# Graph attention layer 0: the three score rows through DRAM instead of TensorE transposes, and ScalarE in source order

## The chip, the cores and the metric

The kernel runs on one core of a Trainium2 chip. A core has TensorE (matmuls, written PE in the profile), VectorE (DVE), ScalarE (ACT), GpSimd (POOL) and SyncE (SP, which here only issues DMA transfers). The metric is the device time of one execution in microseconds; before the change it is 3209.09 us, the median of three runs (3208.32 to 3210.53).

## The reference

The input is x of shape 32 x 512 x 512 in float32 and one 512 x 512 adjacency matrix shared by all 32 batch elements. Two layers follow each other, and each is added to its input and layer-normalised:

```
layer 0:  h = x W                                    (512 x 256)
          e[i,k] = leakyrelu(h[i].a0 + h[k].a1, 0.2) - 1e9 (1 - adj[i,k])
          x = layernorm(x + concat(softmax(e) h, h))
layer 1:  q, k, v = x Wq' + bq, x Wk' + bk, x Wv' + bv     (8 heads of 64)
          scores = q k' / 8, minus infinity where adj is 0
          x = layernorm(x + (softmax(scores) v) Wo' + bo)
```

What matters here is layer 0: its 512 x 512 score matrix is a sum of a column and a row, built from two numbers per node, h.a0 ("self") and h.a1 ("neighbour").

## The kernel before

A batch element is called a problem below. A tile has 128 partitions; the 512 nodes of a problem are four blocks of 128 nodes (index i or j), so a vector over the nodes is a column of shape 128 x 4. Everything is float32 but the masks, which are bfloat16.

For each problem b the loop at the end of the function goes through four head pairs (hp 0 to 3). In each, `head_scores` (called for the four query blocks) multiplies q and k into PSUM (`ps`, L547), VectorE adds the mask and takes the row maximum in one instruction (`minus_max`, L287), and ScalarE takes the exponential (L556). `head_blocks` transposes 32 x 32 blocks on VectorE (L302), takes the reciprocal of the sums (L565), writes these to DRAM (`d_tot`, L567), reads them back broadcast (`inv`, L570, issued by GpSimd) and issues 16 transfers on SyncE that finish the transposition (`pt` from `t`, L319). `head_values` of the head pair before then multiplies with v (`pav`, L582) and VectorE scales the result (`ot`, L590). `project_two` makes q and k of two head pairs (`pw`, L457, with seven products in place of eight, and ScalarE copies `p1`, `p5`, `p7`, `u2` into buffers of the tag "p"), `project_v` makes v (`pv`, L239, copied out at L530), and `finish` multiplies with Wo (`pf`, L603).

Between those pieces of layer 1 for problem b stand the pieces of layer 0 for b + 1 and b + 2:

- `l0_project(b + 2, i)`, in hp 3: h of one block of nodes, with self and neighbour as its first two columns (`ph`, L239; copied by ScalarE at L339).
- `l0_scores(b + 1)`, in hp 0 between query blocks 1 and 2. `row_of` (L326) turns the column of neighbours into a row that stands on all partitions: four TensorE transposes of a column broadcast to 128 x 128, into PSUM (`pn`). VectorE reduces it four times with mask0 (`junk`, L287), and two tiny instructions make `most` (L360, L361), an upper bound of each node's scores. Four more transposes make the row of selfs (`pself`). ScalarE takes leaky ReLU of row plus column (L366), and GpSimd adds the transposed mask (L370).
- `l0_rows(b + 1)`, in hp 0 behind `head_values`: four transposes make the row of `most` (`pl`).
- `l0_weights(b + 1)`: VectorE subtracts that row (L383), ScalarE takes the exponential (L384).
- `l0_values(b + 1, i)`, in hp 1: the weights times h (`po`, L391), and so on to the layer norm and the transposed x1 of the next problem.

The order of the work on TensorE, SyncE and VectorE is that of the source, by this line:

```
ctx.enter_context(tc.manual_schedule(engines={mybir.EngineType.PE, mybir.EngineType.SP, mybir.EngineType.DVE}))
```

ScalarE's and GpSimd's instructions are ordered by a planner of the framework, by its own estimates. An engine works through its queue in order and waits at an instruction whose inputs or buffers aren't ready. A pool gives each tag a number of buffers (`bufs`); a tile waits until one is released. In PSUM, four banks (tag "m") serve all products but the scores, which have four of their own (tag "s"). Tag "p" has ten buffers, "inv" two.

Problem 0's layer 0 runs before the loop, in a startup that also makes the masks (`masks0`: `maskf` in float32 and from it `mask0`), scales and sums the weights (`weight_sums`) and makes the first x1 (`x1_first`). There GpSimd and VectorE share the mask adds.

Of the kernel before, what the change touches and what calls it, by code (L numbers as in the profile page):

```python
# [26 lines left out]
def kernel(  # L27
# [51 lines left out]
    NB = N // P  # L79
    FC = F // P  # L80
    OC = F1 // P
    NP = H // 2
# [11 lines left out]
    ps_m = ctx.enter_context(tc.tile_pool(name="ps_m", bufs=4, space=bass.MemoryType.PSUM))  # L94
    ctx.enter_context(tc.manual_schedule(engines={mybir.EngineType.PE, mybir.EngineType.SP, mybir.EngineType.DVE}))

# [88 lines left out]
    def masks0():  # L185
        maskf = first[:, 4 * F :].rearrange("p (c n) -> p c n", c=NB)
        for c in range(NB):
            nc.vector.tensor_scalar(
                maskf[:, c, :], adj_sb[:, c, :], -1.0, -MASK0, ALU.add, ALU.mult
            )  # L190
            nc.vector.tensor_scalar(
                mask0[:, c, :], maskf[:, c, :], MASK0_MAX / MASK0, None, ALU.mult
            )
        for j in range(NB):
            pm = ps_m.tile([P, N], F32, name=f"pm_{j}", tag="m")
            for i in range(NB):
# [44 lines left out]
    def psum(name):  # L241
        return ps_m.tile([P, N], F32, name=name, tag="m")
# [98 lines left out]
    def l0_add_h(b):  # L341

        h_sb, z = st["h", b], st["x1", b]
        for i in range(NB):
            nc.gpsimd.tensor_tensor(
                z[:, i, F1:], z[:, i, F1:], h_sb[:, i, 2 : F1 + 2], ALU.add
            )

    def l0_scores(b):


        h_sb = st["h", b]
        pn = psum(f"pn_{b}")
        row_of(lambda i: h_sb[:, i, 1:2], pn)
        least = small.tile([P, NB], F32, name=f"least0_{b}", tag="least0", bufs=2)
        for i in range(NB):
            junk = prob.tile([P, N], F32, name=f"junk_{b}_{i}", tag="p", bufs=10)
# [3 lines left out]
        nc.vector.scalar_tensor_tensor(most, most, ALPHA, most, ALU.mult, ALU.max)  # L361
        pself = psum(f"pself_{b}")
        row_of(lambda i: h_sb[:, i, 0:1], pself)
        et = prob.tile([P, NB, N], F32, name=f"et_{b}", tag="et", bufs=1)
        for j in range(NB):
            nc.scalar.activation(  # L366
                et[:, j, :], pself, AF.Prelu, bias=h_sb[:, j, 1:2], alpha=ALPHA
            )
            engine = nc.vector if b == 0 and j >= 2 else nc.gpsimd
            engine.tensor_tensor(et[:, j, :], et[:, j, :], mask0t[:, j, :], ALU.add)  # L370
        st["l0", b] = et, most

    def l0_rows(b):
        _, most = st["l0", b]
        pl = psum(f"pl_{b}")
        row_of(lambda i: most[:, i : i + 1], pl)
        st["pl", b] = pl

    def l0_weights(b):
        et, _ = st["l0", b]  # L380
        pl = st.pop(("pl", b))
        for j in range(NB):
            nc.vector.tensor_tensor(et[:, j, :], et[:, j, :], pl, ALU.subtract)  # L383
            nc.scalar.activation(et[:, j, :], et[:, j, :], AF.Exp)  # L384
# [63 lines left out]
    def project_two(b, s):  # L448
# [30 lines left out]
        def copy(ps, name):  # L479
            t = prob.tile([P, N], F32, name=f"{name}_{b}_{s}", tag="p", bufs=10)  # L480
            nc.scalar.copy(t, ps)
            return t
# [50 lines left out]
    def head_scores(b, hp, i):  # L533
# [17 lines left out]
        for j in range(2):  # L551
            name = f"{b}_{hp}_{i}_{j}"
            p = prob.tile([P, N], F32, name=f"p_{name}", tag="p", bufs=10)
            least = small.tile([P, 1], F32, name=f"least_{name}", tag="least", bufs=6)
# [6 lines left out]
    def head_blocks(b, hp):  # L561
# [5 lines left out]
        nc.sync.dma_start(d.rearrange("j p i -> p j i"), total)  # L567
        inv = act.tile([P, P, NB], F32, name=f"inv_{b}_{hp}", tag="inv", bufs=2)
        for j in range(2):
# [73 lines left out]
    l0_add_h(0)  # L643
    l0_rows(0)
    l0_weights(0)
# [16 lines left out]
    l0_project(1, 2)  # L662
    l0_project(1, 3)
    x1_sums(0, nc.vector)
    project_v(0, 0)
# [3 lines left out]
    for b in range(B):  # L669
        more = b < B - 1  # L670
        for hp in range(NP):
# [27 lines left out]
            else:  # L699
# [4 lines left out]
                if b + 2 < B:  # L704
                    for i in range(NB):
                        l0_project(b + 2, i)
                if b == 0:
                    project_v(1, 0)
# [113 lines left out]
```

## Time and profile before

The profile is of one execution, of 3209.49 us, whose instructions span 3207.7 us.

| | busy us | share of the span | instructions |
|---|---|---|---|
| TensorE matmul | 3163.1 | 99% | 12216 |
| TensorE weight load | 1806.1 | 56% | 12216 |
| VectorE | 2451.1 | 76% | 5665 |
| ScalarE | 1332.1 | 42% | 3026 |
| GpSimd | 759.1 | 24% | 869 |

| what | count | busy us, or time to landing |
|---|---|---|
| `pn`, `pself`, `pl` transposes (L326) | 128 each | 20.8, 19.2, 21.7 |
| leaky ReLU (L366) | 128 | 76.4 |
| VectorE's subtraction of the row (L383) | 128 | 79.2 |
| `pt` from `t`, 128 KB, SyncE | 2048 | 3.4 to land |
| `d_tot` from `tot`, 4 KB, SyncE | 128 | 2.1 to land |
| `inv` from `d_tot`, 128 KB, GpSimd | 256 | 3.8 to land |

The 16 DMA engines were busy about half of the time, and moved 139 GB/s in the mean. The granted TensorE clock was 0.995 of full speed.

How to read it: an engine's line names the source line, the engine, the operation, what it writes and reads ("out<-in", buffer numbers left out), and shapes as partitions x elements. Lines of a timeline begin with the start and the length in us from the start of the span; what stands in brackets at their end is idle time ahead of the instruction and what ended it. TensorE's instructions overlap, so its cost is read from one start to the next. Each logical float32 matmul stands as two instructions.

### The profile page before, as it was taken

To read this page: it belongs to the slowest core of one execution; us is meant where nothing else is said; L and a number is where in the kernel's file an instruction comes from. 1 tells how busy PE (TensorE), PEld (TensorE's weight loads), DVE (VectorE), ACT (ScalarE), POOL (GpSimd) and SP (SyncE) were. 2 spreads that over 40 slices of the span, in tenths; PEclk is the share of its full clock that TensorE was granted. 3 is DMA by queue.
4 is the path that set the end of the run, shared out by engine and by line. 5 is a ranking of instruction groups with operands and counts; after the bars stand their busy time and mean duration, and the time that the engine had idled before them with its cause. 6 is when DMAs were issued, how large, how long until landed. Compare 5 with 4: busy or idle time off the path is not lost.

```text
span 3207.7 us, 41188 instructions
## 1 busy us (share of the span) xinstructions
PE 3163.1 (99%) x12216; PEld 1806.1 (56%) x12216; DVE 2451.1 (76%) x5665; ACT 1332.1 (42%) x3026; POOL 759.1 (24%) x869
## 2 busy tenths in 40 slices
PE   7999999999999999999999999999999999999997
PEld 5555555556556555555565565555555655655543
DVE  5788777877777877778777778877787777788775
ACT  3444443434444444434344444444343444444432
POOL 1322222221222222222222222222222122222210
PEclk9999999999999999999999999999999999999999
DMA  5565555555556555555555555555555555555554
GB/s 148 129 157 127 139 141 150 129 144 143 142 129 152 148 127 137 143 150 128 140 146 141 129 150 149 127 139 141 150 129 145 142 141 129 152 146 128 125 137 115
DMA packets 226094, 446.12 MB, mean 139 GB/s; under 512 B 81680, under 2 KB 84240, under 8 KB 225872
## 3 DMA queue, kind: packets, MB, share of 16 engines
q1 hardware_dynamic: 213408, 409.65, 50.5%
q0 software_dynamic: 12464, 33.84, 4.0%
q8 instruction: 99, 1.62, 0.2%
q14 instruction: 123, 1.01, 0.1%
HBM read 108.27 MB, written 34.08 MB: 44 GB/s over the span
## 4 chain that ended last, share of the span: by engine, by line
PE 95%; DVE 1%; SPq 1%; DMA 0%; issue 0%; ACT 0%; DVEq 0%; ACTq 0%
PE pw L457 25%; PE ps L547 15%; PE pav L582 14%; PE pv L239 14%; PE pf L603 13%; PE ph L239 7%; PE po L391 7%; SPq L319 1%; PE pl L326 1%; PE pn L326 1%; DVE t L302 0%; PE pself L326 0%; DMA pt<-t 0%; DVE p L287 0%; DVE x1t_b L302 0%
## 5 line engine op out<-in xcount | busy, mean ns | idle before, releaser
L556 ACT ACTIVATE p<-p,least 128x512 f32<-128x512 f32 x1024 | 725.9, 710 | 485.1 <-DVE least L287 416.4
L287 DVE CUSTOM_DVE_ANT_0 p<-ps,mask 128x512 f32<-128x512 f32 x1024 | 643.0, 684 | 314.0 <-PE ps L547 314.0
L302 DVE STREAM_TRANSPOSE t<-p 128x512 f32<-128x512 f32 x1024 | 621.8, 674 | 0.0
L547 PE MATMUL ps<-qk 64*128 64x512 f32 x2048 | 511.6, 615 | 2.4 <-DVE least L287 2.4
L582 PE MATMUL pav<-pt,v 128*64 128x512 f32 x2048 | 467.7, 598 | 5.3 <-DMA pt<-t 2.7
L603 PE MATMUL pf<-wo_sb,ot 128*128 128x512 f32 x1024 | 459.6, 602 | 5.6 <-DVE ot L590 5.6
L239 PE MATMUL pv<-wv_sb,x1t 128*128 128x512 f32 x1024 | 451.3, 593 | 0.0
L570 POOL DMA_DIRECT2D inv<-d_tot x256 | 134.4, 528 | 1296.2 <-DMA d_tot<-tot 712.2
L603 PEld LDWEIGHTS pf<-wo_sb,ot 128*128 128x128 f32 x1024 | 190.0, 191 | 272.4 <-issue 264.4
L547 PEld LDWEIGHTS ps<-qk 64*128 64x128 f32 x2048 | 177.8, 186 | 265.3 <-issue 207.5
L582 PEld LDWEIGHTS pav<-pt,v 128*64 128x64 f32 x2048 | 136.5, 136 | 321.1 <-issue 250.2
L239 PEld LDWEIGHTS pv<-wv_sb,x1t 128*128 128x128 f32 x1024 | 190.1, 191 | 216.0 <-issue 215.9
L239 PE MATMUL ph<-w_sb,xt 128*128 128x258 f32 x1024 | 236.9, 389 | 5.0 <-ACT x1t L422 4.7
L391 PE MATMUL po<-h,et 128*128 128x257 f32 x1024 | 232.6, 385 | 1.6 <-issue 1.6
L239 PEld LDWEIGHTS ph<-w_sb,xt 128*128 128x128 f32 x1024 | 194.8, 193 | 57.0 <-DVE mv L253 22.0
L258 ACT ACTIVATE rstd<-mv,eps 128x4 f32<-128x4 f32 (+1 forms) x70 | 20.8, 297 | 489.3 <-DVE mv L253 487.2
L391 PEld LDWEIGHTS po<-h,et 128*128 128x128 f32 x1024 | 193.4, 191 | 51.8 <-issue 25.4
L370 POOL TENSOR_TENSOR et<-et,mask0t 128x512 f32<-128x512 f32 x126 | 141.6, 1156 | 304.0 <-ACT et L366 304.0
L446 POOL TENSOR_TENSOR x<-x,bo_sb 128x512 f32<-128x512 f32 x128 | 158.4, 1269 | 190.4 <-DVE x1t_b L302 170.6
L493 DVE SCALAR_TENSOR_TENSOR qk<-pw,bqs_sb,p 128x256 f32<-128x256 f32 x128 | 61.6, 481 | 184.2 <-PE pw L457 116.7
L556 ACT ACTIVATION_READ_ACCUMULATOR p<-p,least 128x1 f32 x1024 | 191.2, 187 | 0.0
L252 DVE BATCH_NORM_STATS2 stats<-x 128x6 f32<-128x512 f32 x256 | 177.5, 693 | 13.9
(99 smaller groups left out, 3762.2 us busy)
## 6 DMA issues: line engine op xcount, KB each, us to landing
pt<-t SPq DMA_DIRECT2D x2048, 128.0 KB, 3.4
x<-in_x_dram SPq DMA_DIRECT2D x32, 1024.0 KB, 5.8
inv<-d_tot POOLq DMA_DIRECT2D x256, 128.0 KB, 3.8
xt<-in_xt_dram SPq DMA_DIRECT2D x31, 1024.0 KB, 5.4
x1t<-x1t_b SPq DMA_DIRECT2D x496, 64.0 KB, 2.0
out_dram<-x SPq DMA_DIRECT2D x31, 1024.0 KB, 4.3
d_tot<-tot SPq DMA_DIRECT2D x128, 4.0 KB, 2.1
xt<-in_xt_dram SPq DMA_DIRECT2D x4, 256.0 KB, 7.4
```

Of the source, the lines that this page charges most:

```text
L239: nc.tensor.matmul(ps, lhs(c), rhs(c), start=(c == 0), stop=(c == FC - 1))
L252: nc.vector.bn_stats(stats, z[:, i, :])
L287: nc.vector.tensor_tensor_reduce(out=out, in0=scores, in1=mask, scale=-1.0, scalar=MIN_INIT, op0=ALU.add, op1=ALU.min, accum_out=least,)
L302: nc.vector.transpose(t[:, :, :, i, :].rearrange("p r c q -> p c r q"), src.rearrange("p (c r k) -> p c r k", r=4, k=G),)
L370: engine.tensor_tensor(et[:, j, :], et[:, j, :], mask0t[:, j, :], ALU.add)
L391: nc.tensor.matmul(po, et[:, j, i * P : (i + 1) * P], h_sb[:, j, 2:], start=(j == 0), stop=(j == NB - 1),)
L446: nc.gpsimd.tensor_tensor(z[:, i, :], z[:, i, :], bo_sb, ALU.add)
L457: nc.tensor.matmul(ps[:, k * half : (k + 1) * half], weights(k, c), moving(c), start=start and k == 0 and c == 0, stop=c == FC // 2 - 1, s ...
L547: nc.tensor.matmul(ps, qk[rows, 0, i * P : (i + 1) * P], qk[rows, 1, :], start=True, stop=True)
L556: nc.scalar.activation(p, p, AF.Exp, bias=least, scale=-1.0, accum_out=total[:, j, i : i + 1])
L582: nc.tensor.matmul(po[j * D : (j + 1) * D, :], st["v", b, c][:, head * D : (head + 1) * D], pt[:, :, j, c, :, :].rearrange("p g i q -> p g ...
L603: nc.tensor.matmul(ps, st["ot", b, c][:, i * P : (i + 1) * P], wo_sb[:, c, :], start=(c == 0), stop=(c == FC - 1),)
```

## The change

For problems 1 to 31 the three rows no longer come from TensorE:

- `l0_columns(b)`, new, called right behind the four `l0_project(b, i)`: ScalarE copies the two columns of h into `att` (128 x 2 x 4), SyncE writes them to DRAM (`d_att`) in pieces of 16 bytes (four node blocks beside each other for one partition), and SyncE reads them back broadcast to all partitions into `rows` (128 x 2 x 512, 512 KB). The row's order is therefore q i, partition first, and no longer i q.
- `l0_scores(b)` takes `pn` and `pself` from `rows`. `mask0` is stored with its columns in the order q i, so that VectorE reads neighbours and mask alike from one end to the other; the leaky ReLU reads the selfs with a step of four elements and writes in the old order. At its end `most` is written to DRAM (`d_most`, 512 single numbers) and read back broadcast into `row` (128 x 512, 256 KB), both on SyncE.
- Problem 0 keeps its transposes, with those of `pn` written in the new order, `pself` made ahead of the reductions and `pl` at the end of `l0_scores`. `l0_rows` is gone.
- `l0_weights(b + 1)` stands ahead of `l0_add_h(b + 1)` in hp 0.
- ScalarE joins the engines whose order is that of the source.
- Tag "p" has nine buffers in place of ten, and "inv" one in place of two.

```diff
-    ctx.enter_context(tc.manual_schedule(engines={mybir.EngineType.PE, mybir.EngineType.SP, mybir.EngineType.DVE}))
+    in_order = {
+        mybir.EngineType.PE, mybir.EngineType.SP, mybir.EngineType.DVE,
+        mybir.EngineType.Activation,
+    }
+    ctx.enter_context(tc.manual_schedule(engines=in_order))
...
             nc.vector.tensor_scalar(
-                mask0[:, c, :], maskf[:, c, :], MASK0_MAX / MASK0, None, ALU.mult
+                mask0[:, c, :].rearrange("p (q i) -> p i q", i=NB),
+                maskf[:, c, :].rearrange("p (i q) -> p i q", i=NB),
+                MASK0_MAX / MASK0,
+                None,
+                ALU.mult,
             )
...
+    def l0_columns(b):
+
+        h_sb = st["h", b]
+        att = small.tile([P, 2, NB], F32, name=f"att_{b}", tag="att", bufs=2)
+        nc.scalar.copy(att, h_sb[:, :, 0:2].rearrange("p i k -> p k i"))
+        d = dram.tile([2, P, NB], F32, name=f"d_att_{b}", tag="datt")
+        nc.sync.dma_start(d.rearrange("k p i -> p k i"), att)
+        rows = prob.tile([P, 2, P, NB], F32, name=f"rows_{b}", tag="rows", bufs=1)
+        nc.sync.dma_start(rows, d.partition_broadcast(P))
+        st["rows", b] = rows
+
     def l0_scores(b):
 
 
         h_sb = st["h", b]
-        pn = psum(f"pn_{b}")
-        row_of(lambda i: h_sb[:, i, 1:2], pn)
+        if b == 0:
+            pself, pn = psum("pself"), psum("pn")
+            for i in range(NB):
+                nc.tensor.transpose(
+                    pn.rearrange("p (q i) -> p i q", i=NB)[:, i],
+                    h_sb[:, i, 1:2].to_broadcast([P, P]),
+                    ident,
+                )
+            row_of(lambda i: h_sb[:, i, 0:1], pself)
+        else:
+            rows = st.pop(("rows", b))
+            pself = rows[:, 0].rearrange("p q i -> p i q")
+            pn = rows[:, 1].rearrange("p q i -> p (q i)")
...
-        pself = psum(f"pself_{b}")
-        row_of(lambda i: h_sb[:, i, 0:1], pself)
         et = prob.tile([P, NB, N], F32, name=f"et_{b}", tag="et", bufs=1)
         for j in range(NB):
+            e = et[:, j, :] if b == 0 else et[:, j, :].rearrange("p (i q) -> p i q", i=NB)
             nc.scalar.activation(
-                et[:, j, :], pself, AF.Prelu, bias=h_sb[:, j, 1:2], alpha=ALPHA
+                e, pself, AF.Prelu, bias=h_sb[:, j, 1:2], alpha=ALPHA
             )
...
-    def l0_rows(b):
-        _, most = st["l0", b]
-        pl = psum(f"pl_{b}")
-        row_of(lambda i: most[:, i : i + 1], pl)
-        st["pl", b] = pl
+        if b == 0:
+            row = psum("pl")
+            row_of(lambda i: most[:, i : i + 1], row)
+        else:
+            d = dram.tile([N], F32, name=f"d_most_{b}", tag="dmost")
+            with nc.allow_non_contiguous_dma(reason="512 numbers"):
+                nc.sync.dma_start(d.rearrange("(i p) -> p i", p=P), most)
+            row = prob.tile([P, N], F32, name=f"row_{b}", tag="row", bufs=1)
+            nc.sync.dma_start(row, d.partition_broadcast(P))
+        st["l0", b] = et, row
...
-        inv = act.tile([P, P, NB], F32, name=f"inv_{b}_{hp}", tag="inv", bufs=2)
+        inv = act.tile([P, P, NB], F32, name=f"inv_{b}_{hp}", tag="inv")
...
+    l0_columns(1)
...
+                    l0_columns(b + 2)
...
-                if more:
-                    l0_rows(b + 1)
-                else:
+                if not more:
                     project_v(b, 1)
                 project_v(b, 2)
                 project_v(b, 3)
                 if more:
+                    l0_weights(b + 1)
                     l0_add_h(b + 1)
-                    l0_weights(b + 1)
```

Left out of the diff are the same change of `bufs` from 10 to the constant 9 (PB) at three further places and the use of `row` for `pl` in `l0_weights`.

More of the change, by code (lines that the diff above doesn't have):

```diff
@@ L80 @@
     FC = F // P
+    PB = 9
     OC = F1 // P
@@ L347, in l0_add_h @@
             )
+    def l0_columns(b):
[7 more added lines that the diff above has]
+        st["rows", b] = rows
     def l0_scores(b):
         h_sb = st["h", b]
-        pn = psum(f"pn_{b}")
-        row_of(lambda i: h_sb[:, i, 1:2], pn)
+        if b == 0:
[11 more added lines that the diff above has]
+            pn = rows[:, 1].rearrange("p q i -> p (q i)")
         least = small.tile([P, NB], F32, name=f"least0_{b}", tag="least0", bufs=2)
         for i in range(NB):
-            junk = prob.tile([P, N], F32, name=f"junk_{b}_{i}", tag="p", bufs=10)
+            junk = prob.tile([P, N], F32, name=f"junk_{b}_{i}", tag="p", bufs=PB)
             minus_max(junk, pn, mask0[:, i, :], least[:, i : i + 1])
@@ L370, in l0_scores @@
             engine.tensor_tensor(et[:, j, :], et[:, j, :], mask0t[:, j, :], ALU.add)
-        st["l0", b] = et, most
-    def l0_rows(b):
-        _, most = st["l0", b]
-        pl = psum(f"pl_{b}")
-        row_of(lambda i: most[:, i : i + 1], pl)
-        st["pl", b] = pl
+        if b == 0:
[8 more added lines that the diff above has]
+        st["l0", b] = et, row
     def l0_weights(b):
-        et, _ = st["l0", b]
-        pl = st.pop(("pl", b))
+        et, row = st["l0", b]
         for j in range(NB):
-            nc.vector.tensor_tensor(et[:, j, :], et[:, j, :], pl, ALU.subtract)
+            nc.vector.tensor_tensor(et[:, j, :], et[:, j, :], row, ALU.subtract)
             nc.scalar.activation(et[:, j, :], et[:, j, :], AF.Exp)
@@ L479, in copy @@
         def copy(ps, name):
-            t = prob.tile([P, N], F32, name=f"{name}_{b}_{s}", tag="p", bufs=10)
+            t = prob.tile([P, N], F32, name=f"{name}_{b}_{s}", tag="p", bufs=PB)
             nc.scalar.copy(t, ps)
@@ L552, in head_scores @@
             name = f"{b}_{hp}_{i}_{j}"
-            p = prob.tile([P, N], F32, name=f"p_{name}", tag="p", bufs=10)
+            p = prob.tile([P, N], F32, name=f"p_{name}", tag="p", bufs=PB)
             least = small.tile([P, 1], F32, name=f"least_{name}", tag="least", bufs=6)
@@ L643 @@
     l0_add_h(0)
-    l0_rows(0)
     l0_weights(0)
```

## The prediction

> **What bounds the kernel now.** I read the busy shares first, then the chain that ended last, then TensorE's timeline over one problem (one of the 32 batch elements) in mid-kernel.
>
> ```profile
> PE 3163.1 (99%) x12216; PEld 1806.1 (56%) x12216; DVE 2451.1 (76%) x5665; ACT 1332.1 (42%) x3026; POOL 759.1 (24%) x869
> ...
> PE 95%; DVE 1%; SPq 1%; DMA 0%; issue 0%; ACT 0%; DVEq 0%; ACTq 0%
> ```
>
> TensorE carries 95% of the chain. A repeated group in that chain (the output projection `pw` of the second half) comes back every 98.02 us (2843.55, 2941.57), through almost the whole kernel. So a microsecond off TensorE per problem is a microsecond off the kernel, unless a partner then comes late. The timeline of TensorE (start, length, line, operation) where the rows are made:
>
> ```profile
> 1433.84 1.99 PE L547 MATMUL ps<-qk 64*128 64x512 f32 x8
> 1435.76 0.65 PE L326 MATMUL pn<-ident,h 128*128 128x128 f32 x4
> 1436.24 0.60 PE L326 MATMUL pself<-ident,h 128*128 128x128 f32 x4
> 1436.68 7.03 PE L239 MATMUL pv<-wv_sb,x1t 128*128 128x512 f32 x16
> 1443.64 1.99 PE L547 MATMUL ps<-qk 64*128 64x512 f32 x8
> 1445.56 3.65 PE L582 MATMUL pav<-pt,v 128*64 128x512 f32 x16
> 1449.14 0.65 PE L326 MATMUL pl<-ident,most 128*128 128x128 f32 x4
> 1449.63 7.03 PE L239 MATMUL pv<-wv_sb,x1t 128*128 128x512 f32 x16
> 1456.59 1.99 PE L547 MATMUL ps<-qk 64*128 64x512 f32 x8
> 1458.51 7.21 PE L391 MATMUL po<-h,et 128*128 128x257 f32 x32
> 1465.65 1.99 PE L547 MATMUL ps<-qk 64*128 64x512 f32 x8
> 1467.57 3.65 PE L582 MATMUL pav<-pt,v 128*64 128x512 f32 x16
> ```
>
> No idle time is noted on any of them; starts, not lengths (they overlap), give the cost: pn and pself 1436.68 - 1435.76 = 0.92 us, pl 1449.63 - 1449.14 = 0.49 us, together 1.41 us a problem.
>
> **The skill.** SBUF — State Buffer, section "Door 1", says that an fp32 access which touches each 16-byte line only once pays a penalty. The trace agrees: L590 reads `inv` at that step and takes 1019 ns, against 689 ns for L612. The section "SBUF: two separate sides" there says that VectorE with two SBUF inputs and GpSimd exclude each other for a whole instruction. This too agrees: `most`, four numbers a lane, runs beside the mask adds of GpSimd (1156 ns each), and takes 161 ns at the least but 1079 in the median:
>
> ```profile
> L361 DVE SCALAR_TENSOR_TENSOR most<-most x32: 161/1079/1083, 26.2 to 3008.9; 128x4 f32<-128x4 f32 x32
> ```
>
> DMA: Bandwidth & Descriptors, "Rules for kernel authors", says that a last dimension with gaps costs one descriptor per element: `most` goes out in 512 pieces of 4 bytes. No transfer of before shows that.
>
> **The change, part by part** (times in the frame of the problem above).
>
> 1. Rows off TensorE: 12 transposes a problem, 1.41 us, for problems 1 to 31. Problem 0 keeps them.
>
> 2. Columns out, rows in. The copy into `att` joins ScalarE behind the last h copy (1514.18 + 0.37), a tiny copy of some 0.3 us: 1514.9. SyncE then writes 256 pieces of 16 bytes, the form of d_tot:
>
> ```profile
> d_tot<-tot SPq DMA_DIRECT2D x128, 4.0 KB, 2.1
> ```
>
> 2.1 us alone, up to 6.4 if it queues behind the output store issued just ahead of it (4.3 us). The 512 KB read takes between 3.4 us (pt, 128 KB) and 5.8 us (x, 1 MB). Rows are there at 1520.4 to 1527.1; the first reader (junk, L287) of the next round is due at 1437.45 + 98.02 - 1.41 = 1534.1. Queued behind on SyncE is d_tot, due at 1424.67 + 98.02 = 1522.7; the read is issued by 1522 even in the bad case. Cost 0, covered by 7 us. (The four new issues of parts 2 and 3 take SyncE 0.37 to 0.59 us each, in stretches where it only waits: 1511.6 to 1522.7 and 1436.2 to 1451.4.)
>
> 3. The row of `most`. It is ready at 1441.65 (1442.5 if the junk reductions, now with two SBUF inputs, lose one turn to GpSimd). The write is worth 2.1 us (like d_tot) to 4.2 (twice the pieces, each as dear); the read 3.4 to 3.8 us (pt, inv). Trip 5.5 to 8.0, I take 6.5: row at 1449. VectorE subtracts it after the transposes (1452.03 before, 1451.1 after, since its scores come 0.92 earlier) and the `ot` product: from 1452.1. Covered by 3 us; and TensorE needs the first exponentials only at 1457.1, so the row may land as late as 1455.0, a trip of 13.3 us. d_tot (due 1451.4) queues behind the read on SyncE, which is issued by 1446.5.
>
> 4. ScalarE reads pself with a 16-byte step: between 672 ns as now and 672 x 1019/689 = 990 ns; I take the upper. Four: +1.3 us, ending at 1442.2 instead of 1440.9; its next real wait ends at 1442.8 (second v copy). Cost 0. VectorE's junk and subtract read contiguous SBUF: 690 ns (L228) against 686 and 680 now.
>
> 5. ScalarE in source order. First place: the four Exp of the weights now stand behind both v copies, just ahead of po. Problem 1, run in the startup, already has that order before. ScalarE, then TensorE:
>
> ```profile
> 90.27 0.58 ACT L530 COPY v<-pv 128x512 f32<-128x512 f32 x1 [2.85 <-PE pv L239]
> 90.75 2.19 ACT L384 ACTIVATE et<-et 128x512 f32<-128x512 f32 x4
> ...
> 92.08 7.21 PE L391 MATMUL po<-h,et 128*128 128x257 f32 x32
> ```
>
> There po starts 1.92 us behind ps, lasts 7.21 and the next ps comes 9.06 us after the first, exactly as in mid-kernel (1456.59 to 1465.65). So it costs 0, but the margin is some 0.2 us (fourth Exp done 2.8 us after ps started, wanted at 3.0).
> Second place: the square root of store(), now behind four exponentials instead of ahead. It moves from 1506.77 to 1511.6 (exponentials from 1507.4, 4 x 0.705, one table load of 1.28). VectorE's reciprocal and four norms end at 1514.1, its next scores come at 1515.23. Cost 0, margin 1.1 us. For problem 30 TensorE has no 7.2 us of ph there: the transposes slip by 2.9 us, pt lands at about 3104 where pav stands at 3103.35: +0.6 us.
> Third place: the startup. Scaling wq now follows the Exp, on which VectorE's weight sums wait:
>
> ```profile
> 25.38 2.20 ACT L221 ACTIVATE wq_sb<-wq_sb 128x512 f32<-128x512 f32 x4
> 28.40 2.43 ACT L384 ACTIVATE et<-et 128x512 f32<-128x512 f32 x4 [0.82 <-DVE et L383]
> ...
> 30.15 0.68 DVE L228 TENSOR_TENSOR wqx_sb<-wq_sb 128x512 f32<-128x512 f32 x1
> ```
>
> 30.83 + 4 x 0.53 = 33.0 instead of 30.15: 2.85 us, on VectorE, which is busy without pause until 47.83 and then releases TensorE. Given back: 0.19 and 0.95 us of its waits there (the last rstd no longer stands behind an h copy), perhaps more. I take +1.5 us (0.9 to 2.9).
>
> 6. What does not gain. pav of the first head pair waits for pt, which lands about 14.0 us after the transposes end, at 1466.0, against 1467.57. The transposes come 0.92 earlier, pav 1.41: margin 1.1, enough. In the first problem VectorE is unbroken from 74.72 to 88.5 and pav at 102.67 is released by pt: there the 1.41 us, and 2.9 us of waiting for `most`, bring nothing; the lost turn of part 3 costs 0.7. In the second, VectorE is also unbroken (164.13 to 178): 0.6 of 1.41 us remains.
>
> 7. Edits without cost: nine p buffers (eight probabilities and one junk live at once; the copies of project_two take freed ones, VectorE being in order anyway); one inv buffer (its refill waits for `ot`, done 1.1 us after the reciprocal, while d_tot lands 2.1 after); mask columns (problem 0 only, under 1 us on VectorE, beside ph). If the p cover went, copies of 0.58 us would wait for transposes of 0.61.
>
> **Sum.** 29 x 1.41 = 40.9, + 0.6, - 0.7 - 1.5 - 0.6 = 38.7 us. The profiled execution took 3209.49 us (span 3207.7): 3170.8. It is 0.4 above the median of the runs, 3209.09; so 3170.4, call it 3170.
>
> **Rivals.**
> Partial gain. One of the thin margins (0.2 us at po, 1.1 at pav and at the norms) goes, and TensorE waits 0.3 to 1.1 us in each of 30 problems. For: their sum of small errors; the second place depends on my table-load order. Against: problem 1 shows po unhurt. 3170 + 9 to + 33: 3179 to 3203, middle 3188.
> Nothing gained: the wait equals 1.41 us, as VectorE behind the lost turns to GpSimd and a late pt would make it: 3203 to 3215. Against: VectorE idles 3.15 us ahead of 1444.80.
> Slower. The row's trip: 512 pieces of 4 bytes into DRAM, then a broadcast. Every us over 13.3 is a us on TensorE; at 14.8 us the gain is gone, from 15.0 it is slower by over 0.2%; at 16.5 us, 30 x (3.2 - 1.41) = 54 us more, about 3263. For: such pieces are unseen here, and loads in the crowded startup took up to 18.6 us to land. Against: the rings are nearly idle from 1441 to 1452, and d_tot, as small, needs 2.1.
> More gained: the startup costs nothing and the first two problems gain theirs: 3155 to 3163.
> That the rows stay on TensorE is excluded: the code for b > 0 has no transpose.
>
> **Numbers.** Likeliest 0.62 (3163 to 3178), partial 0.18, nothing 0.05, slower 0.09, more 0.06. 0.2% is 6.4 us, about what a measurement of this kernel can tell from no change. Faster 0.62 + 0.18 + 0.06 = 0.86, same 0.05, slower 0.09. From 3161 to 3196 lie the likeliest, most of partial and a part of more: 0.8.
>
> **What will show it.** The period 96.61 instead of 98.02; pn, pself and pl at 4 transposes each; TensorE's idle time ahead of po and pav unchanged. Step 3: row landed before 1452 in this frame. Step 4: et from rows at 0.99 us. Step 5: the first ph after x1t some 1.5 us later than 48.53. I am wrong if the subtraction waits for the row, if po waits for Exp, or if pav waits for pt in every problem.

## The result: slower, 3244 us where 3170 were predicted

| kernel | median of the runs | range | against before |
|---|---|---|---|
| before | 3210.53 us | 3208.32 to 3212.12 (5 runs) | |
| after | 3244.27 us | 3242.37 to 3245.52 (5 runs) | 1.0105, 95% interval 1.009 to 1.012 |

The change makes the kernel 1% slower: 34 us, where a gain of 39 was forecast. The time lies far outside the range of 3161 to 3196. It is the rival called "Slower", the row's trip, to which the prediction gave 0.09. The profiled span grew by 36.0 us, from 3207.7 to 3243.7.

The page of after, busy shares and the chain that ended last:

```profile
span 3243.7 us, 40485 instructions
PE 3150.3 (97%) x11844; PEld 1766.2 (54%) x11844; DVE 2458.6 (76%) x5665; ACT 1409.9 (43%) x3057; POOL 760.8 (23%) x869
...
PE 73%; DMA 14%; DVE 8%; issue 1%; SPq 1%; ACT 1%; DVEq 0%; ACTq 0%
PE pw L490 24%; PE pf L636 13%; PE pav L615 11%; PE ps L580 10%; DMA d_most<-most 9%; PE po L424 7%; PE ph L249 7%; DMA row<-d_most 5%; DVE junk L297 2%; DVE p L297 2%; DVE most L393 1%; DVE most L392 1%; PE pv L249 1%; DVE et L416 1%; ACT et L417 1%
```

TensorE's instructions have gone from 12216 to 11844. The 372 that are missing are 31 problems x 12 transposes (a transpose stands as one instruction), as meant. But TensorE's part of the chain fell from 95% to 73%, and DMA, which had none, holds 14%: 9% the write of `most`, 5% its read. These 14% are not time lost: the chain runs along what ended last, and TensorE works beside the transfers for most of their length. The same view in mid-kernel, one round of it in order of time (start, length, what):

```profile
1464.77 1.10 DVE most L393
1465.86 0.02 issue
1465.88 9.07 DMA d_most<-most
1474.95 0.02 issue
1474.97 5.33 DMA row<-d_most
...
1480.39 0.70 DVE et L416
...
1481.17 0.64 ACT et L417
...
1481.86 7.72 PE po L424 x32
1489.57 1.92 PE ps L580 x8
```

Here the row takes 9.07 + 5.33 = 14.4 us from `most` until it can be subtracted. The prediction took 6.5 and let 13.3 pass. TensorE's timeline (start, length, and in brackets the idle time ahead), first the `po` of problem 1, then the same stretch as above, from the `pw` one period earlier to the next:

```profile
100.76 9.49 PE L424 MATMUL po<-h,et 128*128 128x257 f32 x32 [11.75 <-ACT et L417]
...
1396.82 1.13 PE L490 MATMUL pw<-x1t,wq_sb 128*128 128x256 f32 x4
...
1459.44 7.13 PE L249 MATMUL pv<-wv_sb,x1t 128*128 128x512 f32 x16
1466.50 1.99 PE L580 MATMUL ps<-qk 64*128 64x512 f32 x8
1468.42 3.65 PE L615 MATMUL pav<-pt,v 128*64 128x512 f32 x16
1472.01 7.13 PE L249 MATMUL pv<-wv_sb,x1t 128*128 128x512 f32 x16
1479.07 1.99 PE L580 MATMUL ps<-qk 64*128 64x512 f32 x8
1481.86 7.72 PE L424 MATMUL po<-h,et 128*128 128x257 f32 x32 [0.80 <-ACT et L417]
1489.50 1.99 PE L580 MATMUL ps<-qk 64*128 64x512 f32 x8
...
1495.01 1.13 PE L490 MATMUL pw<-x1t,wq_sb 128*128 128x256 f32 x4
```

Three things are to be read from the mid-kernel lines. `po` starts 1481.86 - 1479.07 = 2.79 us behind `ps`, where it took 1.92 before: 0.87 us late. It then takes 1489.50 - 1481.86 = 7.64 us to the next `ps`, where it took 7.14 (1465.65 - 1458.51): another 0.50 us, since the four exponentials now come at the pace of four subtractions that have only just begun. And each `pv` takes 7.06 us (1466.50 - 1459.44) where it took 6.96 (1443.64 - 1436.68): 0.10 us, twice, now that it follows `ps` or `pav` directly and no transpose stands between. (Experiment 2 below, which keeps the transposes of `pl`, has both cases in one round: 1435.99 - 1428.92 = 7.07 us for the `pv` behind `ps`, 1448.94 - 1441.98 = 6.96 for the one behind `pl`.) So the transposes' going is worth 1.41 - 0.20 = 1.21 us, and the row's lateness costs 1.37 in this round: a loss of 0.16. The period shows it, 1495.01 - 1396.82 = 98.19 us between two starts of `pw`, against 98.02.

This round is a mild one. The groups of after that the change touches (busy us, mean ns of one, idle time just before and what ended it):

```profile
L424 PE MATMUL po<-h,et 128*128 128x257 f32 x1024 | 253.6, 402 | 52.3 <-ACT et L417 50.8 <-issue 1.6
...
L397 ACT ACTIVATE et<-rows,h 128x512 f32<-128x512 f32 x124 | 141.9, 1216 | 0.0
...
L297 DVE CUSTOM_DVE_ANT_0 junk<-rows,mask 128x512 f32<-128x512 f32 x124 | 78.3, 688 | 0.0
L416 DVE TENSOR_TENSOR et<-et,row 128x512 f32<-128x512 f32 x124 | 77.4, 687 | 153.3 <-DMA row<-d_most 153.3
...
L392 DVE TENSOR_TENSOR most<-h,least 128x4 f32<-128x4 f32 x32 | 32.9, 1029 | 1.2
```

VectorE stood 153.3 us before the subtractions, 4.9 us a problem, always for the row; TensorE 50.8 of its 52.3 us before `po`, for the exponentials behind them. The DMA issues of after (KB each, median us to landing):

```profile
rows<-d_att SPq DMA_DIRECT2D x31, 512.0 KB, 3.9
row<-d_most SPq DMA_DIRECT2D x31, 256.0 KB, 5.5
...
d_att<-att SPq DMA_DIRECT2D x31, 4.0 KB, 4.5
d_most<-most SPq DMA_DIRECT2D x31, 2.0 KB, 9.0
```

Where the 36.0 us of span lie, from the starts of `pw` in the two traces:

| stretch | `pw` starts at its end, before and after | us | granted clock, before and after |
|---|---|---|---|
| startup | 61.38, 62.98 | +1.6 | 0.89, 0.89 |
| problem 1 | 106.25, 115.68 | +7.8 | 0.96, 0.87 |
| from there to problem 2's layer 0 | 150.69, 161.45 | +1.3 | 1.00, 0.96 |
| problem 2 | 196.85, 214.37 | +6.8 | 1.00, 0.94 |
| the other 29, and the end | | +18.5, some 0.6 a problem | |

Problem 1 is the worst. `most` comes at 83.53 us there, and `po` could start at 88.95, 1.92 us behind a `ps` at 87.03, but starts at 100.76: 11.8 us of the trip of 8.78 + 6.79 = 15.6 us fall on TensorE. That is the wait of 11.75 in the first line of the timeline above.

Not all of the 36.0 us is the row's. In problem 2 `po` takes 9.74 us (199.13 to 208.87) at a granted clock of 0.73, against 7.64 at 1.00 in the round above; the 1.3 us behind problem 1 are lost at 0.96 (1.00 before); one later round (1940.13 to 1992.49) has 0.97, and TensorE is busy for 50.5 us in it where it is for 49.0 in its neighbours. These three make some 5 us, by an estimate from these figures. Whether TensorE's longer waits bring the clock down was not tried.

### The profile page after: what moved, and what is told of

Its sections match the earlier page's. It is cut to its first block, busy times and chain, and to the rows that moved or that the text cites. A ratio compares the mean times of both kernels' runs of the same rounds, so it can differ in the third digit from the quotient of the medians.

```text
span 3243.7 us, 40485 instructions
## 1 busy us (share of the span) xinstructions
PE 3150.3 (97%) x11844; PEld 1766.2 (54%) x11844; DVE 2458.6 (76%) x5665; ACT 1409.9 (43%) x3057; POOL 760.8 (23%) x869
## 3 DMA queue, kind: packets, MB, share of 16 engines
q8 instruction: 95, 1.56, 0.2%
## 4 chain that ended last, share of the span: by engine, by line
PE 73%; DMA 14%; DVE 8%; issue 1%; SPq 1%; ACT 1%; DVEq 0%; ACTq 0%
PE pw L490 24%; PE pf L636 13%; PE pav L615 11%; PE ps L580 10%; DMA d_most<-most 9%; PE po L424 7%; PE ph L249 7%; DMA row<-d_most 5%; DVE junk L297 2%; DVE p L297 2%; DVE most L393 1%; DVE most L392 1%; PE pv L249 1%; DVE et L416 1%; ACT et L417 1%
## 5 line engine op out<-in xcount | busy, mean ns | idle before, releaser
L424 PE MATMUL po<-h,et 128*128 128x257 f32 x1024 | 253.6, 402 | 52.3 <-ACT et L417 50.8
L416 DVE TENSOR_TENSOR et<-et,row 128x512 f32<-128x512 f32 x124 | 77.4, 687 | 153.3 <-DMA row<-d_most 153.3
```

What stands on the lines that cost most here:

```text
L424: nc.tensor.matmul(po, et[:, j, i * P : (i + 1) * P], h_sb[:, j, 2:], start=(j == 0), stop=(j == NB - 1),)
```

## The experiments

Three explanations stood at first. A: the write of 512 pieces of 4 bytes is slow for its small pieces. B: it is not the trip but ScalarE in source order, which brings the exponentials late. C: the DMA rings are busy at this place, and any write and read there would take so long. Beside experiments 1 to 4 the kernel before took 3211.22 us.

**1. `most` written as it lies.** 128 pieces of 16 bytes in place of 512 of 4; the row then has the order q i, and VectorE subtracts it with a step of four.

```
-            d = dram.tile([N], F32, name=f"d_most_{b}", tag="dmost")
-            with nc.allow_non_contiguous_dma(reason="512 numbers"):
-                nc.sync.dma_start(d.rearrange("(i p) -> p i", p=P), most)
-            row = prob.tile([P, N], F32, name=f"row_{b}", tag="row", bufs=1)
+            d = dram.tile([P, NB], F32, name=f"d_most_{b}", tag="dmost")
+            nc.sync.dma_start(d, most)
+            row = prob.tile([P, P, NB], F32, name=f"row_{b}", tag="row", bufs=1)
             nc.sync.dma_start(row, d.partition_broadcast(P))
+            row = row.rearrange("p q i -> p i q")
...
-            nc.vector.tensor_tensor(et[:, j, :], et[:, j, :], row, ALU.subtract)
+            e = et[:, j, :] if b == 0 else et[:, j, :].rearrange("p (i q) -> p i q", i=NB)
+            nc.vector.tensor_tensor(e, e, row, ALU.subtract)
```

> The changed kernel, with most written as it lies (128 pieces of 16 bytes) and the row read in the order q i, so that VectorE subtracts it with a step of four. Theory A (the write of 512 pieces of 4 bytes, 9.0 us to land, makes the row late): the write lands in about 2.3 us like d_tot, TensorE's wait for Exp ahead of po goes from 52 us to under 5, the four subtractions take 3.8 us instead of 2.5 and hide, time 3175 to 3182. Theory B (ScalarE's source order is what costs): time stays within 3235 to 3247. Theory C (the DMA rings are busy there, whatever the pieces): the write still takes 6 us or more, time 3215 to 3245.

Measured: 3178.51 us (3177.32 to 3179.54), ratio 0.9894, interval 0.988 to 0.9909. Its DMA issues, and its timeline of TensorE in mid-kernel:

```profile
row<-d_most SPq DMA_DIRECT2D x31, 256.0 KB, 4.1
d_most<-most SPq DMA_DIRECT2D x31, 2.0 KB, 1.4
```

```profile
1408.62 1.13 PE L491 MATMUL pw<-x1t,wq_sb 128*128 128x256 f32 x4
...
1442.45 1.99 PE L581 MATMUL ps<-qk 64*128 64x512 f32 x8
1444.37 7.21 PE L425 MATMUL po<-h,et 128*128 128x257 f32 x32
1451.51 1.99 PE L581 MATMUL ps<-qk 64*128 64x512 f32 x8
...
1505.43 1.13 PE L491 MATMUL pw<-x1t,wq_sb 128*128 128x256 f32 x4
```

The write lands in 1.4 us instead of 9.0, the trip is 5.5, and `po` starts 1.92 us behind `ps` as before the change, 9.06 us from `ps` to `ps`. The period is 1505.43 - 1408.62 = 96.81 us: exactly 98.02 - 1.21. The rest of the change is untouched here, source order on ScalarE too, so B can't be what made the kernel slower, and this one edit takes 66 us away. It changes the order of the row too, and with it VectorE's subtraction, but that becomes slower and not faster (experiment 8). The read has become shorter as well, 4.1 us against 5.5, though it moves the same bytes.

**2. The row of `most` back on TensorE**, the other two rows still by DRAM:

```
...
-            row = prob.tile([P, N], F32, name=f"row_{b}", tag="row", bufs=1)
-            nc.sync.dma_start(row, d.partition_broadcast(P))
+        st["l0", b] = et, most
+
+    def l0_rows(b):
+        et, most = st["l0", b]
+        row = psum(f"pl_{b}")
+        row_of(lambda i: most[:, i : i + 1], row)
         st["l0", b] = et, row
...
+                if more:
+                    l0_rows(b + 1)
...
```

> The changed kernel, with the row of most made by four TensorE transposes behind head_values as in the kernel before; pn and pself still come from DRAM. Theories A and C (the row's trip is the loss): no wait ahead of po, 0.82 to 0.92 us a problem gained on the kernel before, less 1.6 us of startup: 3184 to 3190. Theory B: the loss stays, 3235 or more.

Measured: 3189.53 us (3187.77 to 3190.28), ratio 0.9928, interval 0.9913 to 0.9943; period 1511.92 - 1414.72 = 97.20. The change without the row of `most` thus gains 0.82 us a problem: 0.92 for `pn` and `pself` less 0.10 at `pv`. The row of `most`, sent in a form that lands in time, adds 97.20 - 96.81 = 0.39.

**3. ScalarE in source order alone**, on the kernel before:

```
-    ctx.enter_context(tc.manual_schedule(engines={mybir.EngineType.PE, mybir.EngineType.SP, mybir.EngineType.DVE}))
+    ctx.enter_context(tc.manual_schedule(engines={mybir.EngineType.PE, mybir.EngineType.SP, mybir.EngineType.DVE, mybir.EngineType.Activation}))
```

> The kernel before with ScalarE in source order and nothing else. Theories A and C: only the startup (about 1.6 us later) and problem 30 (0.6 us) pay: 1.5 to 3 us more than the kernel before. Theory B: 30 us or more above it.

Measured: 3213.22 us (3211.88 to 3217.21, 12 runs), ratio 1.0005, interval 0.9996 to 1.0014. In mid-kernel the order costs nothing: the period is 98.02 us (1423.98 to 1522.00). In the startup VectorE's weight sums wait for the scaling of wq as the prediction said (2.85 us there), and the first `pw` starts at 63.78 us instead of 61.38. In the total these 2 us are not clear of the noise. The timeline of VectorE in this run:

```profile
30.11 0.16 DVE L646 TENSOR_SCALAR bqs_sb<-bq_sb 128x4 f32<-128x4 f32 x1
32.97 0.69 DVE L228 TENSOR_TENSOR wqx_sb<-wq_sb 128x512 f32<-128x512 f32 x1 [2.69 <-ACT wq_sb L221]
```

**4. As many pieces, four times as long.** 512 pieces of 16 bytes: each number of `most` is written four times. The row is read from a quarter of that and holds other numbers, so that another number is subtracted ahead of the exponential.

```
...
+            most4 = small.tile([P, NB, 4], F32, name=f"most4_{b}", tag="most4", bufs=2)
+            nc.vector.tensor_copy(most4, most.unsqueeze(2).to_broadcast([P, NB, 4]))
+            d = dram.tile([4, P, 4], F32, name=f"d_most_{b}", tag="dmost")
+            nc.sync.dma_start(d.rearrange("i p k -> p i k"), most4)
+            row = prob.tile([P, P, 4], F32, name=f"row_{b}", tag="row", bufs=1)
+            nc.sync.dma_start(row, d[0].partition_broadcast(P))
+            row = row.rearrange("p q k -> p (q k)")
```

> The changed kernel, but each number of most is written four times beside itself, so that the write has 512 pieces of 16 bytes instead of 4 (the row then holds other numbers, so the output is not the reference's; one small VectorE copy is added). If the number of pieces sets the 9.0 us: the write lands in 8 to 10 us and the time stays at 3238 to 3248. If their size of 4 bytes does: it lands in 2.5 to 4.5 us and the time falls to 3175 to 3190.

Measured: 3182.21 us (2 runs), ratio 0.9906, interval 0.9886 to 0.9926; the write lands in 2.7 us, the read in 3.3. So it is not the number of pieces that makes the 9.0. It isn't C either: the same queue at the same place carries four times the bytes in under a third of the time. What remained of A was "4 bytes" itself, and that turned out not to be quite it.

**5, 10 and 11. Single numbers, but apart.** The next runs (kernel before: 3209.80 us for 5 to 8, 3211.32 for 9 to 11, 3211.50 for 12) ask whether a piece of 4 bytes is dear, or 4-byte pieces that lie side by side. Each of the 512 numbers gets 64 bytes of DRAM for itself:

```
-            d = dram.tile([N], F32, name=f"d_most_{b}", tag="dmost")
+            d = dram.tile([NB, P, 16], F32, name=f"d_most_{b}", tag="dmost")
...
-                nc.sync.dma_start(d.rearrange("(i p) -> p i", p=P), most)
+                nc.sync.dma_start(d[:, :, 0].rearrange("i p -> p i"), most)
...
-            nc.sync.dma_start(row, d.partition_broadcast(P))
+            nc.sync.dma_start(row, st["d_att", b][0].rearrange("p i -> (p i)").partition_broadcast(P))
```

> The kernel after, with its 512 pieces of 4 bytes written 64 bytes apart in DRAM instead of side by side, and the row taken from d_att, so that nothing waits for the write (the row holds other numbers; the mask of the weights is then not the reference's). Read from it: the time from issue to landing of d_most. If it is the size of 4 bytes as such: still 8 to 10 us, as in the kernel after (9.0). If it is that neighbouring pieces, carried by different DMA engines, fall into the same stretch of DRAM: 2.5 to 4.5 us, as for the 512 pieces of 16 bytes (2.7). The total tells nothing between the two (3176 to 3186 in both, as nothing waits for the write).

(In this kernel, and in the next two, the number that is subtracted ahead of the exponential is not the reference's, but the masks are; and the read of the row goes out right behind the write, without waiting for it.) Measured, in the DMA issues of the kernel with 64 bytes:

```profile
d_most<-most SPq DMA_DIRECT2D x31, 2.0 KB, 1.9
```

512 pieces of 4 bytes in 1.9 us (1.8 to 3.0 in the 31 problems). So a 4-byte piece is not slow, and experiment 4 did not show what it seemed to: with 16 bytes a piece, there were also fewer pieces to a stretch of DRAM. Two further runs take 8 and 16 bytes in place of 64 (a last dimension of 2 and of 4 in place of 16).

> As the run with the 512 pieces of 4 bytes 64 bytes apart, but 8 bytes apart, so that 8 pieces in place of 1 lie in each 64 bytes of DRAM (16 in the kernel after); the row is again taken from d_att and nothing waits for the write. If what counts is how many pieces lie in the same stretch: 3 to 5 us from issue to landing, near the 3.2 us of the 256 pieces of 8 bytes, of which 8 lie in 64 bytes as well. If only pieces that touch are dear: about 1.9 us, as 64 bytes apart.

Its DMA issues:

```profile
d_most<-most SPq DMA_DIRECT2D x31, 2.0 KB, 4.4
```

> The same with the 4-byte pieces 16 bytes apart: 4 of them in each 64 bytes. If what counts is how many pieces lie in the same stretch of 64 bytes: 2.2 to 3 us, as for the 512 pieces of 16 bytes (2.7). If only pieces that touch are dear: about 1.9 us.

Its DMA issues:

```profile
d_most<-most SPq DMA_DIRECT2D x31, 2.0 KB, 2.9
```

All writes of `most` in this study, by how many pieces lie in 64 bytes of DRAM:

| pieces | in 64 bytes | us to landing | kernel |
|---|---|---|---|
| 512 of 4 bytes, side by side | 16 | 9.0 | after |
| 512 of 4 bytes, 8 apart | 8 | 4.4 | 10 |
| 256 of 8 bytes, side by side | 8 | 3.2 | 8 |
| 512 of 4 bytes, 16 apart | 4 | 2.9 | 11 |
| 512 of 16 bytes, side by side | 4 | 2.7 | 4 |
| 128 of 16 bytes, side by side | 4 | 1.4 | 1 |
| 512 of 4 bytes, 64 apart | 1 | 1.9 | 5 |

With the pieces kept at 512 of 4 bytes, landing goes 1.9, 2.9, 4.4, 9.0 as 1, 4, 8, 16 of them share 64 bytes: some 0.35 us for each further piece up to eight, and more beyond. Each of the three spaced kernels ran once, but has 31 writes, from 1.8 to 3.0 us, 2.3 to 3.3 and 3.3 to 5.4. The number of pieces counts too, but for less: with four to 64 bytes, 128 pieces take 1.4 us, the 256 of `d_tot` 2.1 and 512 take 2.7. "Only pieces that touch are dear" falls with the two runs at 8 and 16 bytes. The Trainium skill, DMA: Bandwidth & Descriptors, "Specifications", says that a transfer under 512 bytes makes the DMA engine read, modify and write. Pieces that have to take turns at one stretch of DRAM for that would give this picture, but no run here shows the turns themselves, and 64 bytes is only the widest spacing tried: how long the stretch is stays open. The three totals (3176.99, 3177.73 and 3177.66 us, one run each) say nothing of the write, since nothing waits for it in these kernels.

**8. Pieces of 8 bytes.** Halfway: `most` in 256 pairs, the row in an order that VectorE reads with a step of two.

```
...
+            d = dram.tile([2, P, 2], F32, name=f"d_most_{b}", tag="dmost")
...
+                nc.sync.dma_start(
+                    d.rearrange("h p t -> p h t"), most.rearrange("p (h t) -> p h t", h=2)
+                )
+            row = prob.tile([P, 2, P, 2], F32, name=f"row_{b}", tag="row", bufs=1)
             nc.sync.dma_start(row, d.partition_broadcast(P))
+            row = row.rearrange("p h q t -> p h t q")
...
```

> The kernel after with most written in 256 pieces of 8 bytes, the row kept in that order, and VectorE's subtraction reading it with a step of two. If the time of the write follows the size of a piece smoothly: 4 to 6 us to land, trip 8 to 11 us, under the 13.3 us that the prediction found, so 3176 to 3182. If anything under 16 bytes is as dear as 4: 8 to 10 us to land for half the pieces or about 4.5 if each piece costs the same, with 3185 to 3240 in the first case. The subtraction: about 690 ns if two hits to each 16 bytes are enough for full speed, about 1080 if any step is dear.

Measured: 3177.52 us (3175.5 to 3178.21), ratio 0.9893, interval 0.9878 to 0.9908; not to be told from experiment 1. The write lands in 3.2 us, faster than either theory had it. The group of its subtraction:

```profile
L422 DVE TENSOR_TENSOR et<-et,row 128x512 f32<-128x512 f32 x124 | 77.1, 683 | 0.1
```

and that of experiment 1:

```profile
L417 DVE TENSOR_TENSOR et<-et,row 128x512 f32<-128x512 f32 x124 | 126.2, 1082 | 0.0
```

With a step of two the subtraction runs at full speed (687 ns with no step, in after); with a step of four it takes 1082. The Trainium skill, SBUF — State Buffer, "Door 1", says just this: two hits to a 16-byte line are needed. In experiment 1 the 0.4 us x 4 are hidden behind `pv`: its `po` starts 1.92 us behind `ps`.

**6. The order given back to the planner**, on experiment 1:

```
         mybir.EngineType.PE, mybir.EngineType.SP, mybir.EngineType.DVE,
-        mybir.EngineType.Activation,
```

> The kernel with most written as it lies (128 pieces of 16 bytes), and ScalarE not held to source order. If source order on ScalarE is worth nothing to the rows by way of DRAM (part 5 of the prediction: cost 0 in mid-kernel, +1.5 us in the startup): 3175 to 3180, against 3178.5 with it. If the rows by way of DRAM need it, because the planner puts the att copy or the step-of-four reads where they hold up Exp or the copies of v: over 3185, with waits ahead of po or pav in the trace.

Measured: 3234.92 us (3233.46 to 3235.61), ratio 1.0072, interval 1.0055 to 1.0089. The first theory falls. Without source order on ScalarE, even the row that lands in 5.5 us gives a kernel that is slower than before. Its chain in mid-kernel (start, length, what):

```profile
1429.54 4.06 DMA rows<-d_att
...
1433.62 0.99 ACT et L396
...
1438.85 4.49 POOL et L400 x4
1443.34 1.23 POOL p L542
1444.57 0.02 issue
1444.59 1.67 DVE qk L526 x4
1446.26 0.04 issue
1446.31 1.99 PE ps L580 x8
```

The planner starts the four leaky ReLU as soon as the rows have landed, ahead of and between ScalarE's copies of `pw`, and GpSimd's four mask adds (4.49 us) ahead of its addition of p5 and p7. For that addition `qk` waits, and for `qk` TensorE. The group of `ps` on the page of experiment 6 has the price:

```profile
L580 PE MATMUL ps<-qk 64*128 64x512 f32 x2048 | 517.0, 620 | 56.6 <-DVE qk L526 54.2
```

In experiment 1 the same group waits 2.4 us in all, for `least`. The 54.2 us are nearly the whole of the 56.4 between experiments 6 and 1. In source order the leaky ReLU stand behind those copies and behind the exponentials of a query block. So the order, worth nothing on the kernel before (experiment 3), is what the rows by way of DRAM rest on. The waits foreseen in the expectation, ahead of `po` or `pav`, are not there; it is `ps`.

**7, 9 and 12. The startup.** On experiment 1, the scaling of wq stands between the additions of h and the weights' exponentials, and the first two projections of problem 1 ahead of the second weight sums:

```
     l0_add_h(0)
+    scale_wq()
     l0_weights(0)
...
+    l0_project(1, 0)
+    l0_project(1, 1)
     steps(sums)
     masks1()
```

> The kernel with most written as it lies, and the startup rearranged: wq is scaled ahead of the weights' exponentials again, and the first projections of problem 1 stand ahead of the second weight sums. If the startup loss that the prediction put at 1.5 us (3rd place of its part 5) is the place of the scaling: first product of the second half at 61.3 to 62.0 us instead of about 63, total 3176 to 3177.5 against 3178.5. If that loss lies in the loads of the startup: unchanged within 0.5 us, 3178 to 3179.

Measured: 3175.30 us (3171.82 to 3178.22), ratio 0.9887, interval 0.9872 to 0.9902. The first `pw` (the first product of layer 1) starts at 60.51 us instead of 62.40: earlier even than expected. In experiments 1, 2, 4, 5, 8, 10 and 11, which have the startup of after, it lies between 62.40 and 63.76, so this gain is clear of their scatter; which of the two edits brings it was not tried. In the total, 0.9887 against 0.9894 with overlapping intervals is no proof. Together with the 8 bytes:

> The write of most in 256 pieces of 8 bytes together with the rearranged startup. If the two gains are independent (3177.5 with the 8 bytes alone; the startup brought the first product of the second half from 62.4 to 60.5 us and the total from 3178.5 to 3175.3, with the kernel before 1.4 us lower too): 3174 to 3177, the fastest kernel of this study. If the startup's gain is lost again in problem 1, where the first exponentials are late whatever comes ahead of them: 3177 to 3179.

Measured: 3178.53 us (3176.65 to 3179.48), ratio 0.9899, interval 0.9883 to 0.9916. Nothing of the gain was there, because in this kernel the scaling stood ahead of the whole startup, and not where experiment 7 had it. ScalarE then waited for the load of wq with everything else behind it (timeline of that kernel):

```profile
21.48 2.19 ACT L229 ACTIVATE wq_sb<-wq_sb 128x512 f32<-128x512 f32 x4 [19.46 <-DMA wq_sb<-in_wqt_dram]
```

The first `pw` came at 65.80 us. With the scaling in its place:

> The write of most in 256 pieces of 8 bytes, and the startup as in the run that rearranged it: wq is scaled between the additions of h and the exponentials of the weights. In the run before this one, which was to be this, the scaling had come to stand ahead of the whole startup, and ScalarE waited there until wq had landed. If the place of the scaling is what the startup is sensitive to: first product of the second half at 60.5 to 61.5 us again, total 3173.5 to 3176. If the landing of the loads makes the difference between such runs: no better than 3177.5.

Measured: 3173.19 us (3171.81 to 3177.82), ratio 0.9884, interval 0.9868 to 0.9901, first `pw` at 60.59. Between these two kernels only the place of the scaling differs: 5.2 us at the first `pw`, and 5.3 in the medians, whose intervals overlap. In source order, a place on ScalarE is a promise that its input has landed. Experiment 12 has the lowest median of the study, 1.2% under before and 2.2% under after (3173.19 / 3244.27 = 0.978); against experiments 1, 7 and 8 its lead lies within the intervals.

## Why the prediction was wrong

**Step 3 failed, in the term "the write is worth 2.1 us to 4.2".** It measured 9.0 in the median. The lower end was that of `d_tot`, the upper end "twice the pieces, each as dear". Both ends were worked out from bytes and the number of pieces. Twice the pieces of `d_tot`'s form do stay in that range, 2.7 us in experiment 4. What carries the time to 9.0, by experiments 1, 4, 5, 10 and 11, is how many of them lie together in DRAM, and `d_tot` has 4 in 64 bytes where `d_most` has 16. The transfer in the trace of before that looked nearest was near in bytes and count and far in this.

The second term, 3.4 to 3.8 us for the read, measured 5.5; in experiment 1 it is 4.1 and in 4 it is 3.3. The lateness needs it too: 9.0 + 3.8 = 12.8 us would have stayed within 13.3. In after, the transfers of `pt` are issued 1 to 2 us behind the read (at 1475.95 in the round shown), where in experiments 1 and 4 the row has landed before they come. But `pt` can't be the whole of it: in the problems where the write took over 10 us, the read behind it took only 3.3 to 4.4, with `pt` as close. What sets the read stays open; the two together took 14.2 to 16.0 us in every problem.

Two of the prediction's own signs of being wrong came: the subtraction waits for the row, and `po` waits for the exponentials.

**The deadline of step 3 was right, in part by luck.** 13.3 us was worked out; the trip of 14.4 made `po` 0.87 us late, so 13.5 would have done. But from the row to `po` it took 1481.86 - 1480.30 = 1.56 us where 2.1 had been allowed (1457.1 - 1455.0), and the 13.3 was counted from 1441.65, where `most` would be ready without the turn lost to GpSimd; in after it came 0.5 us later. The two make up for each other. What the rule "every us over 13.3 is a us on TensorE" lacked is the second loss, 0.50 us a round, as `po` then runs at the pace of the subtractions. By the rule, 14.4 us would have left a gain of 0.3 us a round.

**The forecast of the "Slower" rival has the mechanism, the place and the sign.** Its points of decision (14.8 and 15.0 us) were a little too long, for the reason just given and for the next: at 14.4 the gain is already gone. (The middle of the "Partial gain" rival, 3179 to 3203, is 3191 and not 3188, and `pw` is the product for q and k, not the output projection; nothing rests on either.)

**Step 1 was mis-sized: 1.41 us, measured 1.21.** The starts in the trace of before gave the cost of the transposes, but not that each `pv` takes 0.10 us longer where no transpose stands ahead of it. 29 x 0.20 = 5.8 us of the forecast could not be had.

**Step 4 was mis-sized: 990 ns, measured 1216** for the leaky ReLU with a step of four (672 before). The ratio 1019/689 is VectorE's and was carried over to ScalarE, where it is 1.81. (The source moved from PSUM to SBUF as well; no run parts the two.) It is hidden, as predicted.

The groups of after also show what step 4 and step 3 had right: `junk` from SBUF takes 688 ns (690 predicted), and the first `most` instruction loses a turn to GpSimd, 1029 ns in the mean where it had 538.

**Step 2 was right**: the columns land in 4.5 us (2.1 to 6.4 predicted) and the rows in 3.9 (3.4 to 5.8), and nothing waits for them. **Step 5 was right in its sizes**, but for the smallest: the exponentials behind both copies of v leave `po` unhurt wherever the row is in time (experiment 1), VectorE idles 1.15 us between the norms and its next scores there (1.1 predicted), and the startup lost 1.6 us (1.5 predicted; 1.0 to 2.4 in experiments 1 to 5, so the closeness is partly luck). The 0.6 us at problem 30 are not in after (44.88 us against 44.89 between the starts of the last two groups of `pw`); experiments 1 to 3 lose 1.5 to 1.9 there. What step 5 did not see is that the order is needed: costed at "0" as a thing apart, it is worth 56 us to steps 2 and 4. **Step 6** said that problems 1 and 2 together gain nothing (- 0.7 and + 0.6 us); with the late row, and the lower clock in them, they lose 14.6 of the 36.0 us.

Put together, in spans: the prediction had -40.3 us for the 29 problems, problem 30 included, and they brought +18.5, which is 59 of the error of 75; problems 1 and 2, with the 1.3 us between them, brought +15.9 where +0.1 was expected, which is nearly all the rest. (Those 1.3 us are not the row's: experiment 1 has them too, 153.48 - 107.70 = 45.78 us from `pw` to `pw` against 44.44. They are the clock's. It was granted at 0.96 in this stretch in after and in experiments 1, 2, 6, 7, 10 and 11, which take 45.6 to 46.1 us, at 0.93 in experiment 4, which takes 47.8, and at 1.00 in before and in experiments 3, 5, 8, 9 and 12, which take 44.4.) With the write mended (experiment 1) the span falls by 30.9 us of the 38.7 predicted, and of the 7.8 that are missing 5.8 are the 0.20 us at `pv` and 1.3 the clock's.

## What to carry to other kernels

Before a column goes to DRAM as single numbers, ask which numbers lie side by side there and in how many pieces they arrive: let a partition's numbers stay together, and let the reader take the odd order, two elements to each 16 bytes if that can be had. The transfer in a profile that another is best priced by is the one with the same layout in DRAM, not the one with the same size. And an edit that costs nothing alone may be what another edit stands on: try it out of the company of the first before calling it idle.

## What the runs showed of the hardware that was not expected

- 512 pieces of 4 bytes into DRAM: 9.0 us side by side (after), 4.4 at 8 bytes' distance (experiment 10), 2.9 at 16 (11), 1.9 at 64 (5).
- ScalarE, reading 512 float32 from SBUF with a step of 16 bytes: 1216 ns (after), against 672 from PSUM without a step (before); VectorE's subtraction 1082 (experiment 1) against 687 (after), and 683 with a step of 8 bytes (experiment 8).
- `pv` behind `ps` or `pav` with no transposes between takes 0.10 us more (7.06 us in after against 6.96 in before).
